# Layers 0 and 1 of a four-layer graph network: the second half's weight products as seven half products per pair of tiles, statistics on ScalarE, a bias added by transfers

## The chip, the cores and the metric

The kernel runs on one core of a Trainium2 chip, in float32. The metric is the device time of one execution, in microseconds (us); less is better. One launch computes everything, and nothing is computed on the host but the reordering of inputs.

## The reference

Four layers run one after the other on `x` (2708 x 512) with one adjacency matrix `adj` (2708 x 2708, positive weights with the diagonal set). Each layer normalizes, mixes the rows by the matrix, multiplies by a 512 x 512 weight and adds the result to `x`:

```
h = relu(layernorm(x));  x = x + relu(norm(adj + I) @ h @ W0)            # layer 0
h = relu(layernorm(x));  x = x + (norm(adj) @ h @ W1.T + b1)             # layer 1
h = relu(layernorm(x));  x = x + relu(norm(adj + I) @ h @ W2)            # layer 2
h = relu(layernorm(x));  x = x + sigmoid(ga * (attn @ h @ Wsa)           # layer 3
                                       + gb * (adj @ h @ Wg + bg))
```

`norm` scales rows and columns by the inverse roots of the row sums; `attn` is a masked softmax over scores of pairs of nodes; `ga`, `gb` are sigmoid gates.

## The kernel before

**Tiles.** The 2708 rows are 20 full tiles of 128 rows (five for each quarter of the rows, `KT = 5`) and two tail tiles with what is left, 22 in all (`NT`). The first half `H1` is tiles 0 to 9; the second half `H2` is tiles 10 to 19 and the two tails. `h` holds the normalized rows of all tiles in SBUF. `agg` holds the aggregated rows (matrix times `h`), transposed, for one layer.

**A layer.** `aggregate` runs `outer_product(p)` for p = 1, 7, 2, 4, 6, 5, 3 (a product of quarter blocks with seven products in the place of eight, done twice, once in each other). For each p and each half `u` of the columns it loads four blocks of the matrix (`load_o`, on SP's queue, 847.5 KB each) into places taken from the list `free`, makes sums of them on VectorE (`inner_y`: t1, t2, t4 into three buffers and t3 in place) and of parts of `h` (`inner_x`), and runs seven products of ten matmul instructions on TensorE (`multiply`, lines 541 and 547). `free` is a queue of seven places in `obuf`: each use takes four from its front and puts them back at its end, so the next use begins with those that have been free for longest. `aggregate` calls `epilogue(H1)` ahead of the last outer product and `epilogue(H2)` after it; then the next layer's first outer product follows. That one needs `h` of the tiles in `H1` only.

**The epilogue.** `next_x` goes through the tiles in groups of three. For a tile it loads the kept `x` (`load_x`, line 916, on POOL's queue), multiplies the aggregated tile by the weight (`project`, then `tile_product`: four products of 128x128 by 128x512, line 203, each shown as two instructions), applies scale and ReLU on ScalarE (line 929) or scale and `b1` on VectorE (line 931), adds `x` on VectorE (line 934), writes the new `x` to DRAM (line 935, POOL) and takes mean and variance on VectorE (`stats`, lines 234 and 235). For each group it works out the inverse root (`rstd_of`, lines 239 to 230, with one square root on ScalarE, line 224) and normalizes on ScalarE (line 255). A tail's operand is first gathered by copies on VectorE (line 181) into one of two scratch places `y_places`, which are handed out in turn by `new_y`; the ReLU's output takes one of them too.

**Order.** The framework puts each engine's instructions in an order ahead of time: for each engine the earliest in the program that is ready by its reckoning goes next, so program order is the priority, and work of a later stage fills what it holds to be gaps. On the chip every engine then takes its queue in that order.

**Products by pairs.** Layer 3 has the other form of weight product in `gated`, for both halves. `weights_of_pairs` makes four sums of quarter weights (VectorE, once). For a pair of tiles `sums_of_pair` makes four sums of 128x256 on VectorE (lines 1065 to 1068), and `pair_product` runs seven products of two 128x128 by 128x257 products (line 1077) with one copy on ScalarE (line 1088) and five additions on VectorE (lines 1092, 1098, 1103, 1107, 1110):

```
part(pa, 1); v = copy(pa);  part(pb, 6); u2 = v + pb
part(pa, 2, added);         part(pc, 7); u3 = u2 + pc
part(pd, 5); c22 = u3 + pd
part(pc, 4, added); c21 = u2 + pc
part(pd, 3, added); c12 = u2 + pd
results: first tile [pa, c12], second tile [c21, c22]
```

`v`, `u2`, `u3`/`c21` and `c22` live in `upool` (two buffers for `u2`, one for the others); `pa`, `pc`, `pd` share five PSUM banks (`gates_bank`), `pb` has two of its own.

## Time and profile before

| What | Value |
|---|---|
| Time, median of three runs | 2078.27 us (2078.13 to 2078.53) |
| The profiled execution's own time | 2074.84 us |
| Its span (first to last instruction) | 2073.0 us |
| TensorE busy | 2027.9 us, 98% of the span |
| VectorE busy | 1495.6 us, 72% |
| ScalarE busy | 406.1 us, 20% |
| POOL busy | 202.2 us, 10% |
| Granted TensorE clock | 0.997 |

Engines are PE (TensorE), PEld (its weight load), DVE (VectorE), ACT (ScalarE), POOL and SP; an engine with a q behind it is its queue of transfers. A row of the groups view reads: line, engine, operation, output<-input, shapes, count | busy us in all, mean ns of one | idle time ahead of it and what ended it. Matmul instructions overlap, so that their mean is more than the time from one start to the next. In the windows view each line is a stretch of time in us from the span's start, its length, and the busy time and number of instructions of each engine, then the granted clock and what the transfers did. In the timeline a line is start, duration, engine, line, operation and, in brackets, the idle time ahead and its releaser. Layer 0's epilogue of `H2` begins at 413.16 us, layer 1's at 793.71 us; layer 3's products by pairs of the first half lie from 1489.72 to 1520.67 us.

### The profile page before, as it was taken

How to read it: one execution, taken by the hardware profiler on the slowest of the kernel's cores; microseconds unless marked ns; L12 is line 12 of the kernel's file. 1: busy time of each engine (PE TensorE's matmuls, PEld its weight loads, DVE VectorE, ACT ScalarE, POOL GpSimd, SP SyncE). 2: the span in 40 equal slices, each digit the busy share in tenths (PEclk: the TensorE clock that was granted, in tenths of full speed). 3: DMA queues.
4: the chain of work that ended last, by engine and by line, in shares of the span. 5: the costliest groups of instructions: out<-in, count | busy, mean ns of one | idle time of the engine just before them, and what ended most of it. 6: DMA issues, size and time to landing. Idle time of an engine off the chain costs nothing.

```text
span 2073.0 us, 20307 instructions
## 1 busy us (share of the span) xinstructions
PE 2027.9 (98%) x7338; PEld 1285.3 (62%) x7338; DVE 1495.6 (72%) x2593; ACT 406.1 (20%) x822; POOL 202.2 (10%) x367
## 2 busy tenths in 40 slices
PE   5999999999999999999999999999999999999998
PEld 2566655646666655666664556666677666676665
DVE  4678877756776777766587889967758876677634
ACT  1340001130000010100002130000026434444411
POOL 0111111120000011100002130001011000001012
PEclk9999999999999999999999999999999999999999
DMA  9998595555545444754454565545543333233221
GB/s 368 306 376 256 179 338 188 192 184 178 181 148 182 145 167 145 237 179 160 162 169 145 202 210 201 170 157 178 179 149 116 118 105 104 95 105 118 93 82 52
DMA packets 81332, 363.69 MB, mean 175 GB/s; under 512 B 11616, under 2 KB 16668, under 8 KB 81104
## 3 DMA queue, kind: packets, MB, share of 16 engines
q1 hardware_dynamic: 50672, 245.43, 34.5%
q0 software_dynamic: 30560, 116.97, 17.5%
q8 instruction: 58, 0.95, 0.2%
q14 instruction: 42, 0.34, 0.0%
HBM read 297.39 MB, written 62.19 MB: 173 GB/s over the span
## 4 chain that ended last, share of the span: by engine, by line
PE 88%; DVE 5%; DMA 4%; issue 1%; ACT 0%; POOL 0%; SPq 0%; POOLq 0%; DVEq 0%; ACTq 0%
PE pe L1359 17%; PE pa L541 14%; PE pc L541 14%; PE pd L541 14%; PE po L203 9%; PE pb L541 7%; PE pt L603 3%; DMA obuf<-in_yb_dram 2%; PE pd L1077 2%; PE pa L1077 2%; PE pc L1077 1%; DMA ends<-in_yt_dram 1%; PE pt L608 1%; PE pe L603 1%; PE pb L1077 1%
## 5 line engine op out<-in xcount | busy, mean ns | idle before, releaser
L1359 PE MATMUL pe<-obuf,h 128*128 128x339 f32 x1280 | 373.2, 448 | 0.0
L541 PE MATMUL pa<-obuf,h 128*128 128x339 f32 x1040 | 318.7, 451 | 2.5 <-ACT h L255 1.4
L1359 PEld LDWEIGHTS pe<-obuf,h 128*128 128x128 f32 x1280 | 241.4, 189 | 121.8 <-issue 4.1
L541 PEld LDWEIGHTS pa<-obuf,h 128*128 128x128 f32 x1040 | 196.2, 190 | 110.2 <-issue 10.3
L203 PE MATMUL po<-ends,agg 128*128 128x512 f32 x480 | 207.5, 593 | 0.0
L1225 ACT ACTIVATE e<-r,nsr 128x339 f32<-128x339 f32 x352 | 172.4, 566 | 178.2 <-DVE obuf L1229 87.1
L541 PE MATMUL pb<-t,s 128*128 128x339 f32 x560 | 171.0, 452 | 0.8 <-DVE t L513 0.8
L541 PE MATMUL pc<-t,h 128*128 128x339 f32 x560 | 169.4, 448 | 1.3 <-DVE u L588 1.3
L541 PE MATMUL pd<-t,s 128*128 128x339 f32 x560 | 169.0, 447 | 0.0
L541 PE MATMUL pd<-obuf,s 128*128 128x339 f32 x550 | 166.3, 448 | 1.1 <-DVE s L557 0.8
L575 ACT COPY v<-pa 128x339 f32<-128x339 f32 x56 | 24.7, 441 | 719.0 <-PE pa L541 693.0
L203 PEld LDWEIGHTS po<-ends,agg 128*128 128x128 f32 x480 | 90.9, 190 | 114.3 <-issue 109.5
L541 PEld LDWEIGHTS pb<-t,s 128*128 128x128 f32 x560 | 106.3, 191 | 56.1 <-DVE t L513 2.1
L541 PEld LDWEIGHTS pc<-t,h 128*128 128x128 f32 x560 | 105.8, 189 | 56.3 <-DVE u L588 2.4
L541 PEld LDWEIGHTS pd<-t,s 128*128 128x128 f32 x560 | 105.8, 189 | 54.1
L541 PEld LDWEIGHTS pd<-obuf,s 128*128 128x128 f32 x550 | 104.0, 189 | 54.8 <-DVE s L557 1.3
L541 PE MATMUL pc<-obuf,s 128*128 128x339 f32 x450 | 135.9, 448 | 0.0
L541 PEld LDWEIGHTS pc<-obuf,s 128*128 128x128 f32 x450 | 85.1, 189 | 43.8 <-issue 0.5
L935 POOL DMA_DIRECT2D xs<-ends x66 | 36.0, 545 | 780.9 <-DVE ends L934 702.2
L513 DVE TENSOR_TENSOR t<-obuf,t 128x1695 f32<-128x1695 f32 x55 | 105.2, 1913 | 0.0
L1229 DVE SCALAR_TENSOR_TENSOR obuf<-obuf,e 128x1695 f32<-128x1695 f32 x32 | 61.5, 1923 | 58.8 <-DMA obuf<-in_yb_dram 39.8
L514 DVE TENSOR_TENSOR t<-obuf,t 128x1695 f32<-128x1695 f32 x52 | 99.4, 1912 | 0.5 <-PE pc L541 0.5
(321 smaller groups left out, 2417.4 us busy)
## 6 DMA issues: line engine op xcount, KB each, us to landing
obuf<-in_yb_dram SPq DMA_DIRECT2D x132, 847.5 KB, 4.6
obuf<-osumt SPq DMA_DIRECT2D x100, 847.5 KB, 4.5
osumt<-obuf POOLq DMA_DIRECT2D x22, 847.5 KB, 12.1
xs<-ends POOLq DMA_DIRECT2D x66, 256.0 KB, 2.3
ends<-xs POOLq DMA_DIRECT2D x60, 256.0 KB, 4.1
obuf<-in_yt_dram SPq DMA_DIRECT2D x28, 339.0 KB, 3.6
obuf<-in_yb_dram POOLq DMA_DIRECT2D x11, 847.5 KB, 10.8
ends<-in_yb_dram SPq DMA_DIRECT2D x9, 847.5 KB, 9.4
```

Source lines behind the costliest of these rows:

```text
L203: nc.tensor.matmul(po, cs[c], ws[c], start=(c == 0), stop=(c == NC - 1))
L513: nc.vector.tensor_add(t2, o22, t1)
L514: at_y.append(nc.vector.tensor_add(t4, o21, t2).ins)
L541: last = nc.tensor.matmul(ps, x[:, k, :], y[:, k, :], start=start and k == 0, stop=k == KT - 1, skip_group_check=not start,)
L575: at_v.append(nc.scalar.copy(v, pa).ins)
L603: nc.tensor.matmul(ps[c], h[:, NF, c * P : (c + 1) * P], tl[:, 0, :], start=start, stop=False)
L608: nc.tensor.matmul(ps[c], h[g, NF + 1, c * P : (c + 1) * P], tl[g, 1, :], start=False, stop=True)
L935: nc.gpsimd.dma_start(xs[t], xt)
L1077: nc.tensor.matmul(ps, xs_[k][:, c], ws[k][:, c], start=start and c == 0, stop=c == 1, skip_group_check=not start,)
L1225: nc.scalar.activation(e[:, k], row, AF.Exp, bias=nsr[:, t, s : s + 1], scale=1.0)
L1229: nc.vector.scalar_tensor_tensor(b, b, 0.0, e1[:, :n], ALU.not_equal, ALU.min)
L1359: nc.tensor.matmul(pe[c], h[:, t, c * P : (c + 1) * P], a, start=(t == 0), stop=False)
```

## The change

For layers 0 and 1, and for the second half only, the ten full tiles are projected as five pairs by `next_x_by_pairs`; the two tails go through `next_x` after them, as a group of two. The sums of the weights, the sums of the pairs and one more place for a kept `x` lie in three blocks taken from the front of `free`, which are put back at its end when the epilogue is done. ScalarE takes sum and sum of squares (`stats_by_act`) for all of these tiles in layer 1, and in layer 0 for all but the second tile of every second pair. `b1` is no longer loaded to SBUF and added on VectorE: in layer 1's aggregation 22 transfers on POOL's queue add `b1` to the kept `x` in DRAM (after outer product 1 for `H1`, after 7 for six tiles of `H2`, after 2 for the other six), and in both epilogues of layer 1 the scaled product is added to `x` in one instruction. `weights_of_pairs`, `sums_of_pair` and `pair_product` are unchanged; the function definitions only move in the file.

```diff
+    def places_of_pairs():
+        blks = [free.pop(0) for _ in range(3)]
+        flat = [blk.rearrange("p k w -> p (k w)") for blk in blks]
+        n = 2 * D
+        return (
+            blks,
+            [flat[0][:, k * D : (k + 1) * D] for k in range(3)] + [flat[1][:, 0:D]],
+            [in_four(flat[1][:, D : D + n]), in_four(flat[2][:, 0:n])],
+            flat[2][:, n : n + D],
+        )
+
+    def stats_by_act(xt, mv):
+        y = new_y()
+        nc.scalar.activation(y, xt, AF.Identity, accum_out=mv[:, 0:1])
+        nc.scalar.activation(mv[:, 0:1], mv[:, 0:1], AF.Copy, scale=1.0 / D)
+        nc.scalar.activation(y, xt, AF.Square, bias=mv[:, 0:1], scale=-1.0, accum_out=mv[:, 1:2])
+        nc.scalar.activation(mv[:, 1:2], mv[:, 1:2], AF.Copy, scale=1.0 / D)
+
+    def next_x_by_pairs(ts, w_sb, scale, relu, src, colscale, after=None):
+        nonlocal xt_places
+        blks, w_places, s_places, x_place = places_of_pairs()
+        xt_places = xt_places + [x_place]
+        ws = weights_of_pairs(
+            w_sb.rearrange("p c (k o) -> p c k o", k=2),
+            [a.rearrange("p (c o) -> p c o", c=NC // 2) for a in w_places],
+        )
+        halves = [slice(k * (D // 2), (k + 1) * (D // 2)) for k in range(2)]
+        pairs = [(t, t + 1) for t in ts if t < NF][::2]
+        xs_ = sums_of_pair(pairs[0], s_places)
+        for n, pair in enumerate(pairs):
+            xts = [load_x(t, src) for t in pair]
+            mv = small.tile([P, KT, 2], FP, tag="mv", name="mv")
+            *_, po = pair_product(xs_, ws, gates_bank)
+            if n + 1 < len(pairs):
+                xs_ = sums_of_pair(pairs[n + 1], s_places)
+            for s, (t, xt) in enumerate(zip(pair, xts)):
+                y = new_y()
+                for f, c in zip(halves, po[s]):
+                    if relu:
+                        nc.scalar.activation(y[:, f], c, AF.Relu, scale=scale[:, t : t + 1])
+                    else:
+                        nc.vector.scalar_tensor_tensor(
+                            xt[:, f], c, scale[:, t : t + 1], xt[:, f], ALU.mult, ALU.add
+                        )
+                if relu:
+                    nc.vector.tensor_add(xt, xt, y)
+                nc.gpsimd.dma_start(xs[t], xt)
+                if s == 0 or n % 2 == 0 or not relu:
+                    stats_by_act(xt, mv[:, s, :])
+                else:
+                    stats(xt, mv[:, s, :])
+            rstd = rstd_of(mv, 2)
...
+        xt_places = [p for p in xt_places if p is not x_place]
+        next_x([t for t in ts if t >= NF], w_sb, scale, relu, src, colscale, after)
+        free.extend(blks)
...
     def next_x(ts, w_sb, scale, relu, src, colscale, after=None):
...
-                if bias is None:
-                    nc.scalar.activation(y, po, AF.Relu, scale=scale[:, t : t + 1])
-                else:
-                    nc.vector.scalar_tensor_tensor(
-                        y, po, scale[:, t : t + 1], bias, ALU.mult, ALU.add
-                    )
-                nc.vector.tensor_add(xt, xt, y)
+                if relu:
+                    y = new_y()
+                    nc.scalar.activation(y, po, AF.Relu, scale=scale[:, t : t + 1])
+                    nc.vector.tensor_add(xt, xt, y)
+                else:
+                    nc.vector.scalar_tensor_tensor(
+                        xt, po, scale[:, t : t + 1], xt, ALU.mult, ALU.add
+                    )
...
-    b1_bc = misc[:, 0:D]
-    nc.gpsimd.dma_start(b1_bc, b1.partition_broadcast(P))
-    aggregate(False, lambda ts: next_x(ts, w1_sb, dis, b1_bc, xs, dinv))
+    def add_b1(ts):
+        for t in ts:
+            nc.gpsimd.dma_start(xs[t], b1.partition_broadcast(P), accum_op=ALU.add)
+    aggregate(
+        False,
+        lambda ts: (next_x if ts[0] < half else next_x_by_pairs)(
+            ts, w1_sb, dis, False, xs, dinv
+        ),
+        {p: lambda ts=ts: add_b1(ts) for p, ts in zip((1, 7, 2), (H1, H2[:6], H2[6:]))},
+    )
```

## The prediction

> **What bounds the kernel now.** I read the page first (engines, the 40 slices), then the windows view of the stretches that the change touches, then the timeline around them, and last the groups view, for durations.
>
> ```profile
> PE 2027.9 (98%) x7338; PEld 1285.3 (62%) x7338; DVE 1495.6 (72%) x2593; ACT 406.1 (20%) x822; POOL 202.2 (10%) x367
> ...
> core 0: us, PE busy (x) PEld busy (x) DVE busy (x) ACT busy (x) POOL busy (x), PEclk, DMA share, GB/s
> 413.16:447.50 34.34, 34.34 (x82) 15.20 (x81) 19.92 (x56) 11.24 (x18) 8.01 (x15) 1.00 0.38 132
> 793.71:828.10 34.39, 34.39 (x82) 15.25 (x81) 26.37 (x67) 5.06 (x9) 8.15 (x15) 1.00 0.40 137
> 1489.72:1520.67 30.95, 30.95 (x144) 26.35 (x141) 21.39 (x64) 11.79 (x31) 4.37 (x8) 1.00 0.27 96
> ```
>
> The first two windows are the ten full tiles of `H2` in layers 0 and 1, the third is the ten tiles of layer 3's `gated`, which already go by pairs. TensorE has no gap in either stretch to be changed, at full clock, so only less TensorE work can shorten them. VectorE has 14.4 us free in layer 0 and 8.0 in layer 1, ScalarE 23 and 29. A product stage of 140 short instructions has run once, in 30.95 us, with VectorE at 69%.
>
> ```profile
> 399.57 1.92 DVE L512 TENSOR_TENSOR t<-obuf 128x1695 f32<-128x1695 f32 x1
> 401.53 1.93 DVE L516 TENSOR_TENSOR obuf<-obuf 128x1695 f32<-128x1695 f32 x1
> ...
> 409.24 1.92 DVE L513 TENSOR_TENSOR t<-obuf,t 128x1695 f32<-128x1695 f32 x1
> ...
> 411.49 1.91 DVE L514 TENSOR_TENSOR t<-obuf,t 128x1695 f32<-128x1695 f32 x1
> ...
> 413.36 43.32 SPq L445 DMA_DIRECT2D obuf<-in_yb_dram  x2
> ...
> 1501.62 0.42 DVE L1107 TENSOR_TENSOR u<-u,pc 128x257 f32<-128x257 f32 x1
> 1501.95 0.42 DVE L1138 TENSOR_TENSOR ends<-pa,ends 128x256 f32<-128x256 f32 x1
> ...
> L255 ACT ACTIVATE h<-ends,sh,rstd 128x512 f32<-128x512 f32 x66 | 49.1, 804 | 35.4 <-DVE sh L247 35.1
> L929 ACT ACTIVATE ends<-po,dd 128x512 f32<-128x512 f32 x44 | 30.2, 685 | 169.0 <-PE po L203 167.1 <-PE po L210 1.8
> L286 ACT ACTIVATE y<-h,mv 128x512 f32<-128x512 f32 x12 | 8.7, 723 | 0.3
> L291 ACT ACTIVATE y<-h 128x512 f32<-128x512 f32 x12 | 7.6, 630 | 13.9 <-DMA h<-in_x_dram 13.6
> L224 ACT ACT_TABLE_LOAD x1 | 1.3, 1283 | 0.0
> ```
>
> The first four rows are the sums of the next layer's first outer product, made before this epilogue starts. The SPq row is two of the four loads for its second half. The two rows at 1501 us show that VectorE's 0.42 us operations follow each other every 0.33 us.
>
> **TensorE.** Removed: 80 instructions of 512 columns, 34.34 us, 0.43 each. Added: 140 of 256 columns. Layer 3's took 30.95 us for 257 columns, its own short stalls included; times 256/257 that is 30.8. Gain 3.5 us for a layer, 7.0 for both. With no stall at all (0.2169 from start to start in the timeline, as 0.8675 for four) it would be 30.3, and 8.1 for both: more than that the change can't bring.
>
> **VectorE, layer 0.** For the five pairs: 45 operations of 256 columns (nine a pair) by 0.335 = 15.1; ten additions of `x` (L934, 0.69, next one after 0.61) 6.1; statistics of two tiles left 1.6; five root chains of eight small operations, 0.2 each where each waits for the last and 0.09 where others lie between, 3.6 to 8.0; what is left over from outer product 3 at 413.3 to 415.5, 2.3. Sum 28.7 to 33.1, against 19.9 now and 30.8 of TensorE. Layer 1: 15.1, twenty half tiles by 0.40 (nearest row L1250, 0.48) 8.0, roots 3.6 to 8.0, left over 2.8: 29.5 to 33.9, against 26.4. The four sums of the weights (0.69 each by L934, 2.8) are needed by the second product, but their places have been free since outer product 3's first half, and VectorE is busy only 13.4 of 20 us ahead of 413; I cost them at nothing, and at 2.8 if that cover is gone.
>
> **ScalarE, layer 0.** A pair: the copy `v` 0.3; four half ReLUs, between the copy of 256 columns (0.36) and L255's 256 columns with two operands (0.59), I take 0.37 apart, 1.5; statistics of a tile 0.75 and 0.84 (L291 and L286 with their reads of the sum) and two scalings of 0.2, 2.0; two normalizations at 0.74, 1.5; a root 0.2. That is 7.5 with two statistics and 5.5 with one, 33.5 for five pairs. Some 6 of it fall behind the last product, which leaves 27.5 of 30.8. Layer 1 has no ReLU: 30, of which 24.5 fall inside. So all three engines are nearly full.
>
> **A rule against it.** The chip loaded a table three times in the whole profile; L224's load came with the first square root at 30.6 us, and the sums and squares of 80 to 110 us and every later root, ReLU and copy went on without one. The Trainium skill (ScalarE: Activation LUTs, What ACT_TABLE_LOAD costs) says that every switch to another table set costs some 2.66 us. If Square and Identity were not in the square root's set, each pair would pay two switches, 5.3 us, and ScalarE would pace layer 0 at about 12 us a pair, some 25 us a layer lost. The trace decides: square, then root, without a load, so nothing.
>
> **What moves.** Three blocks leave `free`. The next layer's first half then no longer gets the three that had long been free, but those that outer product 3's second half releases last, the fourth only at 413.2. So t2, t3 and t4 (three of the four rows above, 1.92 each, 5.8 us) move behind 413 into the full VectorE. They are first needed by product `pb` of the next layer, which starts at 456.16 now. The transfers themselves (4.6 us to landing) have 35 us to arrive. The second half's blocks (three behind the last pair, at about 444, on SP in order) are needed by its sums near 462; now too one of them, the second transfer of the SPq row above, is sent only at 456.35; t3 began with it at 464.18 and TensorE never waited. So nothing.
>
> **The tails** now wait: a tail's gather takes a `y` place that the last pair still uses. Behind the last product come c12 0.5, ReLU 0.55, addition 0.8, the second tile's ReLUs 0.9 and addition 0.8, copies 0.9, about 4.5 us, in layer 1 as much through the statistics. TensorE has the next layer's `pa` in hand meanwhile, 2.86 us, and `pb` if t2 is ready. Between 0 and 1.6 us a layer; I take 0.5.
>
> **POOL and transfers.** 22 accumulating transfers of 256 KB. Nearest rows: accumulations of 847.5 KB cost POOL 0.86 us and land in 10.8; plain ones of 256 KB cost 0.54 and land in 2.3 to 4.8. POOL pays 12 to 19 us of its 1870 idle us. Queued behind one that waits are POOL's `x` loads, which have several free places ahead of their use, and the writes of `x`: nothing. Between gain and loss nothing is excluded (the load of `b1` goes away, 5.6 MB of writes come); I take nothing, up to 4 us if they delay matrix blocks.
>
> **H1 of layer 1** saves ten additions, 6.1 us of VectorE, where TensorE is busy 35.00 of 35.00: nothing.
>
> **Sum.** -7.0, plus stalls inside the pairs beyond layer 3's, because VectorE and ScalarE have about 95% to carry: 0 to 2.5 a layer, 0.7 taken, 1.4; plus 1.0 for the tails. -4.6 us. Against the profiled execution, 2074.84 (span 2073.0), that is 2070.2; the median shown, 2078.27, lies 3.4 above that execution, and I carry the difference over: 2073.7. About 0.2%, 4.2 us, is what a measurement can tell from no change.
>
> **The rivals.**
> B: ScalarE paces layer 0. The second tile's ReLU shares a `y` place with the first one's addition, normalizations are older in program order, and `u3` (one buffer) waits until that ReLU has read it; then product 4 waits about 1 us a pair. Layer 0 gives 0, layer 1 2: about 2076.5. For: 33.5 against 30.8. Against: layer 3's trace shows TensorE running 6, 7 and 5 ahead of a late 2.
> C, slower: VectorE becomes the bound. From 413.16 to `pb` it must do 33.1 + 5.8 + 6.3 for the tails (copies, additions, statistics, root), 45.2, and 48 with the weight sums. It decides when this exceeds the 43.0 us that TensorE takes there now. A t of 1.92 us put into a gap of 0.3 holds up the whole queue behind it. Price 2 to 5 us a layer: 2082 to 2088, likeliest 2083. Against: the t's are later in program order, and behind the pairs VectorE was busy only 11.3 of 20 us, so it can catch up.
> D: `b1`'s ten first transfers fall on 452 to 472, where transfers take 0.80 of their engines, and matrix blocks come late: 4 us on top, 2078.
> E: the order does not interleave pairs, and each pair begins with sums after the last addition, 1 us a pair: gain 0 in both layers, 2078. Against: in layer 3 the sums of the next pair stand between the additions of this one.
>
> **How the numbers follow.** The likeliest case 0.54 (its own range 2071 to 2076; 0.46 of it faster, 0.08 within); B 0.16 (0.01 faster, 0.13 within, 0.02 slower); C 0.20, slower; D and E 0.10 (0.07 within, 0.03 slower). Faster 0.47, within 0.28, slower 0.25. The range goes from the stall-free 2070.2 to C's likely value, 2083, and leaves out the worse half of C.
>
> **What would show it.** Right: 140 instructions of 256 columns in 31 to 32.5 us in each layer, TensorE busy throughout, VectorE 29 to 33 us in it, no new table load, `pb` of the next layer 3 us earlier. Wrong: over 34 us with PE waiting for `u` or `s` (VectorE) or `v` (ScalarE); rows L513, L514 or L516 between the pairs' additions; PE waiting for `t` at the next layer's `pb`; blocks from DRAM landing late beside the `b1` transfers.

## The result, and the profile after

The changed kernel takes 2103.97 us (median of four runs, 2101.79 to 2106.65), the kernel before 2078.2, measured beside it: ratio 1.0128, 95% interval 1.0115 to 1.0142. That is 26 us slower where 4.6 us less were forecast, and outside the range. The profiled execution took 2106.65 us, its span is 2104.9 us. The engines on its page:

```profile
PE 2034.0 (97%) x7458; PEld 1311.9 (62%) x7458; DVE 1503.8 (71%) x2675; ACT 442.0 (21%) x954; POOL 221.2 (11%) x388
```

The two profiled executions differ by more than the medians: their spans are 31.9 us apart (2104.9 - 2073.0). TensorE is busy for 6 us more although its matmuls have less to do, and idle for 26 us more (2104.9 - 2034.0 against 2073.0 - 2027.9). The windows view of the two stretches of pairs, from their first product to the one behind their last, layer 0 and layer 1 (start:end, length, then busy time of each engine, granted clock, DMA share, GB/s):

```profile
416.75:454.83 38.08, 35.34 (x153) 28.21 (x152) 31.19 (x85) 23.16 (x67) 10.00 (x15) 1.00 0.55 137
819.18:852.00 32.82, 32.72 (x146) 26.93 (x144) 30.41 (x92) 19.31 (x57) 7.55 (x14) 1.00 0.39 128
```

Each window also holds a few instructions of other products: by the timeline they take 1.7 us of the second (a tail's product) and 3.6 us of the first (the next layer's first products). So layer 1's pairs take 31.1 us, as forecast, and TensorE is idle for 0.1 us there. Layer 0's take 34.5 us, no less than the 34.34 they replace. Neither explains the loss. It is found by cutting the time at the first products of the epilogues: from layer 0's second-half epilogue to layer 1's first-half one, on to its second-half one, and on to layer 2. First three lines of before, then three of after:

```profile
413.16:719.28 306.12, 306.12 (x1068) 190.02 (x1066) 214.14 (x328) 28.85 (x48) 13.72 (x25) 1.00 0.51 170
719.28:793.71 74.43, 74.43 (x224) 41.81 (x221) 53.95 (x108) 8.96 (x16) 10.86 (x20) 1.00 0.48 164
793.71:1104.34 310.63, 309.41 (x1083) 191.62 (x1082) 223.82 (x339) 21.78 (x38) 17.00 (x31) 1.00 0.52 172
```

```profile
416.75:743.53 326.78, 310.49 (x1127) 203.01 (x1126) 226.67 (x372) 45.38 (x113) 24.03 (x36) 0.98 0.56 176
743.53:819.18 75.65, 74.69 (x224) 41.71 (x221) 47.89 (x106) 9.07 (x16) 11.30 (x21) 1.00 0.39 130
819.18:1130.84 311.66, 307.01 (x1144) 203.46 (x1142) 226.88 (x374) 41.17 (x105) 16.35 (x30) 0.99 0.53 179
```

20.7 of the 31.9 us are lost in the first of these, almost all of it behind the pairs, in the tails and layer 1's outer products: TensorE is idle for 16.3 us of the stretch, and the clock falls to 0.98. The other two lose 1.2 and 1.0 us, what follows them 5.4, and what lies ahead of them 3.6. 2.1 of these 3.6 us are one gap that ends at 382.36 us, while the first `b1` transfers run; e2_b1_only (below) has such a gap too, and the kernel before, e1_no_b1 and e5_few_rows have none there. The timeline of TensorE after shows two of the holes (start, duration, engine, line, and in brackets the idle time ahead and who ended it):

```profile
468.65 5.37 PE L203 MATMUL po<-ends 128*128 128x512 f32 x8 [4.51 <-DVE ends L181]
...
485.56 0.94 PE L541 MATMUL pd<-obuf,s 128*128 128x339 f32 x1 [4.60 <-DVE agg L562]
```

Both name VectorE, and VectorE's own timeline passes the blame on to blocks of the matrix that have not landed:

```profile
464.01 1.93 DVE L512 TENSOR_TENSOR t<-obuf 128x1695 f32<-128x1695 f32 x1 [6.00 <-DMA obuf<-in_yb_dram]
...
468.28 0.36 DVE L181 COPY ends<-agg 128x128 f32<-128x128 f32 x2
...
484.37 0.30 DVE L463 SCALAR_TENSOR_TENSOR obuf<-ident,obuf 128x128 f32<-128x128 f32 x1 [8.17 <-DMA obuf<-osumt]
```

And POOL, in the same stretch, stands at the transfers of `b1` (L1105), with the writes of `x` (L1041) and the loads of `x` (L989) behind them:

```profile
445.90 0.84 POOL L1105 DMA_DIRECT2D xs<-in_b_dram  x1 [5.08 <-DMA xs<-ends]
...
462.50 0.85 POOL L1105 DMA_DIRECT2D xs<-in_b_dram  x1 [9.32 <-DMA xs<-ends]
463.06 0.86 POOL L1041 DMA_DIRECT2D xs<-ends  x1
463.61 0.85 POOL L1041 DMA_DIRECT2D xs<-obuf  x1
```

The transfers of `b1`, meant for layer 1's products, were put as early as their data allow: behind each write of `x` in layer 0's epilogue. The last row writes the `x` that lies in a block of `obuf`; that block can be loaded anew only when the write has landed. SP's queue sends the last block of layer 1's first product then:

```profile
469.36 0.33 SPq L445 DMA_DIRECT2D obuf<-in_yb_dram  x1
```

Three more of them go at 449.6, 452.5 and 455.0 us. Before, one block of that product was sent after 414 us:

```profile
456.35 0.33 SPq L445 DMA_DIRECT2D obuf<-in_yb_dram  x1
```

So the first theory was: what costs is the place of these transfers at the head of POOL's queue. Its rivals were the blocks that change hands, the bytes of the transfers, and full engines in the pairs.

### The profile page after: what moved, and what is told of

The parts are those of the page before. It is cut to its first block, busy times and chain, and to the rows that moved or that the text cites. A ratio compares the mean times of both kernels' runs of the same rounds, so it can differ in the third digit from the quotient of the medians.

```text
span 2104.9 us, 20810 instructions
## 1 busy us (share of the span) xinstructions
PE 2034.0 (97%) x7458; PEld 1311.9 (62%) x7458; DVE 1503.8 (71%) x2675; ACT 442.0 (21%) x954; POOL 221.2 (11%) x388
## 3 DMA queue, kind: packets, MB, share of 16 engines
q0 software_dynamic: 33648, 122.48, 19.2%
## 4 chain that ended last, share of the span: by engine, by line
PE 74%; issue 11%; DMA 6%; DVE 5%; POOL 2%; ACT 1%; POOLq 0%; SPq 0%; DVEq 0%; ACTq 0%
PE pe L1435 17%; PE pc L541 12%; PE pa L541 12%; PE pd L541 12%; PE pb L541 6%; PE po L203 4%; PE pt L603 3%; DMA obuf<-in_yb_dram 2%; DMA obuf<-osumt 1%; PE pd L943 1%; PE pa L943 1%; PE pc L943 1%; PE pe L603 1%; PE pt L608 1%; DMA xs<-ends 1%
## 5 line engine op out<-in xcount | busy, mean ns | idle before, releaser
L541 PE MATMUL pa<-obuf,h 128*128 128x339 f32 x1040 | 316.5, 449 | 4.6 <-ACT v L575 3.2
L541 PEld LDWEIGHTS pa<-obuf,h 128*128 128x128 f32 x1040 | 195.8, 190 | 110.3 <-issue 6.9
L541 PE MATMUL pc<-t,h 128*128 128x339 f32 x560 | 171.4, 452 | 6.3 <-DVE u L588 6.2
L541 PE MATMUL pb<-t,s 128*128 128x339 f32 x560 | 172.7, 454 | 2.1 <-DVE s L473 1.3
L541 PE MATMUL pd<-obuf,s 128*128 128x339 f32 x550 | 168.6, 453 | 4.9 <-DVE agg L562 4.9
L575 ACT COPY v<-pa 128x339 f32<-128x339 f32 x56 | 24.5, 438 | 699.8 <-PE pa L541 696.8
L541 PE MATMUL pd<-t,s 128*128 128x339 f32 x560 | 169.4, 448 | 0.0
L541 PEld LDWEIGHTS pc<-t,h 128*128 128x128 f32 x560 | 106.4, 191 | 63.2 <-DVE u L588 9.2
L541 PEld LDWEIGHTS pb<-t,s 128*128 128x128 f32 x560 | 106.4, 191 | 59.1 <-issue 3.1
L541 PEld LDWEIGHTS pd<-obuf,s 128*128 128x128 f32 x550 | 105.0, 192 | 59.9 <-DVE agg L562 6.8
L541 PEld LDWEIGHTS pd<-t,s 128*128 128x128 f32 x560 | 105.8, 189 | 55.0 <-issue 1.3
L203 PE MATMUL po<-ends,agg 128*128 128x512 f32 x320 | 138.6, 593 | 0.0
L541 PE MATMUL pc<-obuf,s 128*128 128x339 f32 x450 | 135.9, 448 | 0.0
L541 PEld LDWEIGHTS pc<-obuf,s 128*128 128x128 f32 x450 | 85.1, 189 | 43.8 <-issue 0.5
L203 PEld LDWEIGHTS po<-ends,agg 128*128 128x128 f32 x320 | 60.5, 190 | 76.6 <-issue 73.9
L513 DVE TENSOR_TENSOR t<-obuf,t 128x1695 f32<-128x1695 f32 x55 | 105.4, 1916 | 0.1
L512 DVE TENSOR_TENSOR t<-obuf 128x1695 f32<-128x1695 f32 x48 | 92.1, 1919 | 14.6 <-DMA obuf<-in_yb_dram 11.6
## 6 DMA issues: line engine op xcount, KB each, us to landing
obuf<-in_yb_dram SPq DMA_DIRECT2D x132, 847.5 KB, 4.5
obuf<-osumt SPq DMA_DIRECT2D x100, 847.5 KB, 4.5
osumt<-obuf POOLq DMA_DIRECT2D x22, 847.5 KB, 11.0
obuf<-in_yb_dram POOLq DMA_DIRECT2D x11, 847.5 KB, 11.1
ends<-in_yb_dram SPq DMA_DIRECT2D x9, 847.5 KB, 9.8
```

Source lines behind the costliest of these rows:

```text
L203: nc.tensor.matmul(po, cs[c], ws[c], start=(c == 0), stop=(c == NC - 1))
L512: nc.vector.tensor_add(t1, o12, o11)
L513: nc.vector.tensor_add(t2, o22, t1)
L541: last = nc.tensor.matmul(ps, x[:, k, :], y[:, k, :], start=start and k == 0, stop=k == KT - 1, skip_group_check=not start,)
L575: at_v.append(nc.scalar.copy(v, pa).ins)
```

## The experiments

The table gives ratios to the kernel before, run beside each. One thousandth is 2.1 us. The ratios, not the medians, are compared between runs. e1, e7, e8, e9 and e12 leave `b1` out and e5 most of it; they are there to part causes.

| Run | What differs | Ratio, 95% interval |
|---|---|---|
| changed | | 1.0128, 1.0115 to 1.0142 |
| e1_no_b1 | changed, no `b1` transfers | 1.0022, 1.0013 to 1.0032 |
| e2_b1_only | before, with the `b1` transfers | 1.0091, 1.0065 to 1.0118 |
| e3_b1_late | changed, transfers behind the last write of `x` | 1.0168, 1.0138 to 1.0198 |
| e4_turned | before, `free` turned by three | 0.9996, 0.9987 to 1.0005 |
| e5_few_rows | changed, transfers cut to 8 rows | 1.0019, 1.0010 to 1.0029 |
| e6_b1_spread | changed, transfers spread over layer 1 | 1.0059, 1.0042 to 1.0077 |
| e7_layer1_only | no `b1`, pairs in layer 1 alone | 1.0008, 0.9999 to 1.0017 |
| e8_no_x_place | no `b1`, no place of `x` in a block | 1.0009, 1.0000 to 1.0019 |
| e9_tails_early | e8, tails behind the first pair | 1.0031, 1.0017 to 1.0045 |
| e10_b1_pool | e9, `b1` added by POOL and VectorE | 1.0048, 1.0035 to 1.0061 |
| e11_layer0_early | e9's pairs in layer 0 alone, layer 1 as before | 1.0034, 1.0021 to 1.0048 |
| e12_one_block | e8, pairs hold one block instead of three | 0.9980, 0.9971 to 0.9990 |
| e13_layer0_one_block | e12's pairs in layer 0 alone, layer 1 as before | 1.0001, 0.9991 to 1.0010 |
| e14_ten_by_transfer | e12, `b1` by ten spread transfers and VectorE | 0.9993, 0.9986 to 1.0000 |

### The transfers of b1: there or not, alone, later

e1_no_b1 takes the hooks out of the changed kernel:

```diff
-        {p: lambda ts=ts: add_b1(ts) for p, ts in zip((1, 7, 2), (H1, H2[:6], H2[6:]))},
```

> The changed kernel without its 22 transfers of b1 (b1 is left out of the computation; everything else stays). My theory: these transfers stand at the head of POOL's in-order queue, each waiting for the write of the x that it adds to, and so hold up the later writes and loads of x, the place of x that lies in a block of obuf, and with it the next layer's blocks. Then about 25 of the 26 us that the change lost come back and the time is 2072 to 2080 us; the start of the first-half epilogue of layer 1, 743.60 us in the changed kernel, goes back to 716 to 722, and TensorE has no gap over 2 us between 414 and 600 us. Rival 1, the blocks: free hands over its places in another order and one place of x lies in a block of obuf, which alone makes the next layer's blocks late; then the gaps at 464, 481 and 505 us stay and the time is 2095 to 2104. Rival 2, bandwidth: only the bytes of b1's transfers count; then 6 to 10 us come back (2094 to 2098), since 11 MB in all are a small share of what is moved. Rival 3, full VectorE and ScalarE in the pairs: less than 5 us come back.

Measured: 2082.3 us, 1.0022. Of 1.0128, 1.06%, or 22 us, are the transfers' doing. The remaining 0.22% (4.6 us) is not: the time lies 2 us above what my theory gave. One gap over 2 us stays between 414 and 600 us, 3.3 us at the tails. The two rivals that leave `b1` out of the cause fall.

e2_b1_only puts the same transfers into the kernel before, without pairs:

```diff
-            y, po, scale[:, t : t + 1], bias, ALU.mult, ALU.add
+            xt, po, scale[:, t : t + 1], xt, ALU.mult, ALU.add
...
+        for t in ts:
+            nc.gpsimd.dma_start(xs[t], b1.partition_broadcast(P), accum_op=ALU.add)
```

> The kernel before with only the b1 part of the change: 22 accumulating transfers on POOL's queue and, in layer 1's epilogues, the scaled product added to x in one instruction; no pairs, no blocks taken from free. My theory: POOL's queue is held up in the second-half epilogue of layer 0 here too, but with the two old places of x outside obuf the blocks do not hang on it, so that part of the loss shows: 5 to 20 us slower than before, 2083 to 2098, with waits of POOL at the transfers of b1 for the writes of x of several us each and x loads late at L916. Rival 1, the blocks alone: within 3 us of before. Rival 2, bandwidth: 6 to 10 us slower.

Measured: 2095.98 us, 1.0091, 19 us. Most of the loss comes without pairs and without a place of `x` in a block, so the chain through that block, which my theory had for a good part of it, isn't needed.

e3_b1_late holds all 22 back behind the last write of `x`:

```diff
+        with tc.issue_after(last_x):
             for t in ts:
                 nc.gpsimd.dma_start(xs[t], b1.partition_broadcast(P), accum_op=ALU.add)
```

> The changed kernel with all its transfers of b1, which are now put behind the last write of x of the layer before in POOL's order; nothing else is changed. My theory: what costs is their place in POOL's queue, not their bytes or their number; then the time is that of the kernel without b1 plus at most 3 us, 2072 to 2082 us, and the start of layer 1's first-half epilogue lies at 716 to 724 us. Rival 1, the blocks: 2095 to 2104, unchanged. Rival 2, bandwidth: the same bytes fall on the same layer, so at least 6 of the 10 us remain: 2082 to 2100.

Measured: 2110.78 us, 1.0168, slower still, and outside all three expectations. My theory falls. POOL's writes and loads of layer 0 were no longer held up (no gap over 1.4 us before 488), but the transfers then ran one behind the other from 470 to 525 us, beside the matrix blocks. The windows view of that time:

```profile
480.00:500.00 20.00, 10.37 (x33) 6.49 (x33) 7.19 (x10) 0.44 (x1) 4.05 (x6) 0.81 1.03 240
500.00:520.00 20.00, 20.00 (x66) 12.91 (x65) 13.00 (x14) 3.24 (x3) 6.40 (x8) 0.94 1.05 162
520.00:540.00 20.00, 11.29 (x34) 7.01 (x32) 8.15 (x10) 0.00 (x0) 4.12 (x7) 0.74 1.06 227
```

The DMA engines are full (share 1.03 to 1.06; before, 0.52 in each of these stretches), and they move no more than 162 to 240 GB/s, where the load of the kernel's first blocks reaches 370 (the rows of the 40 slices). TensorE waited 9.6 and 8.7 us for VectorE's L588, which stood behind late blocks. So the accumulating transfers are dear. The two DMA tables, POOL's queue of the changed kernel and of e1_no_b1 (packets, MB, share of 16 engines):

```profile
q0 software_dynamic: 33648, 122.48, 19.2%
```

```profile
q0 software_dynamic: 30480, 116.71, 17.1%
```

19.2% of 2104.9 us less 17.1% of 2081.1 us is 48 us of all 16 engines for 22 transfers, 2.2 us each (e2_b1_only against before gives 1.8, e6_b1_spread against e1_no_b1 2.3). The rest of this queue moves 116.7 MB in 356 us, 0.8 us for 256 KB. A `b1` transfer takes the engines two to three times as long as this queue's average for the same bytes. No run tells which property makes it so: that it adds, that it goes from DRAM to DRAM, or that its source is one row read 128 times. How much of a packet's time is waiting beside other transfers the traces do not tell either.

### Bytes or queue

e5_few_rows leaves the 22 transfers where they are in POOL's queue, with their waits, and cuts what they carry:

```diff
-            nc.gpsimd.dma_start(xs[t], b1.partition_broadcast(P), accum_op=ALU.add)
+            nc.gpsimd.dma_start(xs[t][0:8], b1.partition_broadcast(8), accum_op=ALU.add)
```

> The changed kernel with each of its 22 transfers of b1 cut to the first 8 of a tile's 128 rows (b1 is left out of the other rows). They stand at the same places of POOL's queue and wait for the same writes of x, but carry 16 KB for 256 KB. Theory Q, POOL's queue: the waits at its head are what costs, so nearly all of the loss stays, 2096 to 2104 us. Theory D, the DMA engines: 256 KB that are accumulated in DRAM take them twice as long as 256 KB that are plainly written (from the queues' shares of before and after, 1.7 us of all 16 engines against 0.8), 37 us in all, in a stretch that has room for half of that; then nearly all of it goes and the time is 2082 to 2088, near that of the kernel without b1 (2082.3).

Measured: 2080.22 us, 1.0019, the same as with no transfers at all, and 2 us below theory D's range; theory Q falls. POOL still stands at them, first the changed kernel's waits, then this one's (us in total, times, longest):

```profile
POOL xs L1105 <- DMA xs<-ends: 91.1, 15, 15.7
```

```profile
POOL xs L1105 <- DMA xs<-ends: 43.5, 14, 8.6
```

43.5 us of waiting at the head of POOL's queue cost nothing that the times show. What the changed kernel pays for is the bytes, that is the time that 256 KB take in the DMA engines. That POOL's longer waits are a consequence of it, since the writes that it waits for land late, fits these rows but was not tested by itself.

e6_b1_spread carries all bytes but one transfer at a time, behind every second matrix block:

```diff
+        t = b1_due.pop(0) if b1_due else None
+        if t is not None:
+            with tc.issue_after(at_sp.ins):
+                nc.sync.dma_start(bs[t][0], b1)
+            with tc.issue_after(at_x[-1]):
+                nc.gpsimd.dma_start(xs[t], bs[t][0].partition_broadcast(P), accum_op=ALU.add)
```

> The changed kernel with its 22 full transfers of b1 spread out over layer 1: the transfer of one tile follows every second matrix block from the first product's second half to the fifth product (each waits for a 2 KB copy of b1 that stands on SP's queue behind that block's load). Theory D: the same 37 us of DMA time then meet 230 us in which the engines are half idle (share 0.52), so the loss goes: 2080 to 2087, as without b1, and the granted clock stays at 1.00 from 490 us on. Theory Q: POOL's queue is held for longer still, the loads of x of layer 1 come late, and the time is 2095 or more.

Measured: 2089.4 us, 1.0059, between the expectations and nearer to theory D's: 14 of the 22 us come back although POOL waits 153.8 us for the copies, and 7.7 stay. The share is 0.74 to 0.80 from 480 to 540 us:

```profile
480.00:500.00 20.00, 17.07 (x54) 10.84 (x53) 12.59 (x18) 1.64 (x2) 3.98 (x6) 0.91 0.74 229
500.00:520.00 20.00, 20.00 (x71) 13.24 (x70) 14.11 (x15) 2.04 (x3) 2.29 (x3) 1.00 0.80 217
```

A block beside such a transfer still comes late now and then (gaps of 2.9 us up to 489.7 and 1.9 up to 616.4, and slower instructions after each). Even spread, the transfers are not free; what the 22 small copies on SP's queue cost, which this run adds, was not measured. Some 2.7 us of the rest lie at the very end of the program (last section).

### What the pairs lose without b1

e4_turned turns the order of places in the kernel before:

```diff
+        if turned:
+            free.extend([free.pop(0) for _ in range(3)])
```

> The kernel before with free turned by three places behind the second-half epilogues of layers 0 and 1, as if three blocks had been taken from its front and put back at its end; nothing else. It shows what the handing on of other places costs by itself. My theory and the prediction: within 2 us of before, 2076 to 2080, with the three sums of 1.92 us of the next layer's first product moved behind the epilogue's start. Rival 1, the blocks: TensorE waits 2 to 5 us a layer for the sums or the second half's blocks, 2082 to 2090.

Measured: 2075.73 us, 0.9996: nothing. The sums moved behind 413 us (L513 now at 418.25) and TensorE did not notice.

e7_layer1_only (without the hooks, and `next_x` for all of layer 0):

```diff
-        (next_x if ts[0] < half else next_x_by_pairs)(ts, w_sb[0], dinv, True, x, dis)
+        next_x(ts, w_sb[0], dinv, True, x, dis)
```

> The kernel without b1, with pairs in layer 1 alone; layer 0's second half goes tile by tile as before (b1 is left out). It parts the 6 us that the kernel without b1 still lies over the kernel before. My theory: in layer 0 the place of x that lies in a block of obuf comes free only when the x is written, the block's load is late by 3 to 5 us, VectorE stands at the sum of that block with the last tile's addition behind it, and the idle TensorE then runs its next 3 us at a lower clock; layer 1 gains 0.4 as it is. So 2074 to 2077 us, 6 to 8 less than the kernel without b1. Rival, VectorE and ScalarE too full in both layers alike: 2078 to 2080. Rival, the pairs gain nothing and the tails cost the same in both: 2079.

Measured: 2079.18 us, 1.0008. Both rivals' figures fit, my theory's do not, and the interval touches both no difference from before and that of e1_no_b1, so the times alone do not part the layers. The profile does: layer 1 to 2 took 312.5 us (310.6 before), with gaps of 2.5 us at the tails and 2.6 behind them. So the fault is not layer 0's alone, as I had it.

e8_no_x_place:

```diff
-        xt_places = xt_places + [x_place]
```

> The kernel without b1 and without the additional place of x in a block of obuf; pairs in both layers (b1 is left out). My theory, the block of the next layer waits for the write of that x: the block's load starts 3 us earlier, at about 453.5 instead of 456.8, the gap of 3.3 us ahead of layer 0's tails goes down to less than 1.5 and the slow clock behind it goes too: 2075 to 2079 us. Rival, the other two blocks are as late (they are held by the last pair's products) or the pairs now wait for places of x: 2081 to 2085.

Measured: 2079.81 us, 1.0009 (the intervals of this and of e1_no_b1 overlap). In the profile the last block of layer 1's first product is sent at 450.2 instead of 456.4 us, and layer 0's gap at the tails is 0.9 for 3.3 us; but layer 1 has one of 3.3 us there, where VectorE stood at a late block before it came to the tail's copies:

```profile
833.37 0.61 DVE L463 SCALAR_TENSOR_TENSOR obuf<-ident,obuf 128x45 f32<-128x45 f32 x3 [2.53 <-DMA obuf<-in_yb_dram]
...
837.20 0.44 DVE L181 COPY ends<-agg 128x32 f32<-128x32 f32 x4 [0.49 <-ACT ends L1009]
```

In the windows view, from each second-half epilogue to the next first-half one, TensorE is idle for 3.6 and 3.8 us:

```profile
412.71:720.76 308.05, 304.50 (x1127) 200.92 (x1126) 224.28 (x368) 45.06 (x113) 13.78 (x25) 1.00 0.52 177
796.03:1106.35 310.32, 306.54 (x1143) 203.20 (x1141) 226.90 (x374) 41.41 (x105) 16.97 (x31) 0.99 0.53 181
```

e9_tails_early asks whether it is the tails:

```diff
+            if n == 0:
+                next_x([t for t in ts if t >= NF], w_sb, scale, relu, src, colscale, after)
...
-        next_x([t for t in ts if t >= NF], w_sb, scale, relu, src, colscale, after)
```

> The kernel without b1 and without the place of x in obuf (b1 is left out), in which the two tails are projected behind the first pair instead of behind the last. It tests what still eats the pairs' gain: there TensorE stood 0.9 us in layer 0 and 3.3 us in layer 1 ahead of the tails (L181), because the copies that gather a tail stood on VectorE behind the sums and loop additions of a block of the next layer that came late, and behind statistics on ScalarE. My theory: both gaps go, and layer 0 from its second-half epilogue to layer 1's first-half one takes 305 to 307 us (306.1 before, 308.05 with the tails last), layer 1 to 2 306 to 308 us (310.6 before, 310.3 with the tails last): 2071 to 2075 us, 0.1 to 0.3% below before. Rival: the late block stops another user of VectorE just as long (the next layer's u2 and u3), and TensorE waits there: 2077 to 2081, no gain.

Measured: 2083.89 us, 1.0031: the rival, and worse than that. The gaps at the tails moved to the next layer's third sum (`u3`, L588), 2.4 us in layer 0 and 4.9 in layer 1. VectorE ahead of it, in layer 1:

```profile
846.81 1.93 DVE L512 TENSOR_TENSOR t<-obuf 128x1695 f32<-128x1695 f32 x1 [1.49 <-DMA obuf<-in_yb_dram]
...
850.60 0.41 DVE L463 SCALAR_TENSOR_TENSOR obuf<-ident,obuf 128x45 f32<-128x45 f32 x2 [1.78 <-DMA obuf<-in_yb_dram]
...
855.85 0.69 DVE L1137 CUSTOM_DVE_ANT_0 ends<-ends 128x512 f32<-128x512 f32 x1 [1.91 <-DMA ends<-in_wsa_dram]
856.54 0.50 DVE L588 TENSOR_TENSOR u<-u,pc 128x339 f32<-128x339 f32 x1
```

VectorE waits for one late block after the other, and whatever is queued behind their sums is late, a tail or a `u3`. The tails were only the first in line. The last wait of the four rows is for no block: it is for a part of layer 3's weight, whose use the order had put ahead of this `u3`. e7_layer1_only has such a wait too, 4.72 us (`in_asa_dram`), ahead of its gap of 2.6 us.

e12_one_block takes the blocks' holder away. The pairs hold one block; the rest of their sums lies in rows of `h` that nobody reads any more:

```diff
-        blks = [free.pop(0) for _ in range(3)]
+        blks = [free.pop(0)]
...
+            [flat[:, n : n + D], h[:, NF], h[:, NF + 1], h[:, NF - 2]],
+            [in_four(flat[:, 0:n]), in_four(hf[:, (NF - 4) * D : (NF - 2) * D])],
```

> The kernel without b1 and without the place of x in obuf (b1 is left out), tails last as in the change, in which the pairs take one block of free instead of three: two sums of weights lie in h of the tails, one in h of tile 18, and the second places of the pairs' sums in h of tiles 16 and 17, all of which are dead until these tiles are normalized. My theory, late blocks: with three blocks the next layer's second half could load its blocks only from the last pair's products on, and TensorE waited behind VectorE for them (3.6 us idle in layer 0 and 3.8 in layer 1 from the second-half epilogue to the next first-half one); with one it loads three of four as early as before, as the kernel before does, so the idle time falls to 1.5 to 2.5 in layer 0 (the 1.4 us stall inside the pairs stays) and under 1 in layer 1: 2070 to 2075 us, 2 to 6 below the one with three blocks. Rival, the tails: the late statistics on ScalarE and the shared places y hold up the gather whatever the blocks do, 3 us in layer 1 stay: 2077 to 2080.

Measured: 2072.82 us, 0.9980 (0.9971 to 0.9990), as expected: by the ratios 6 us less than with three blocks and 4 us less than the kernel before. Two blocks of the next layer's first product are sent only near the end of the pairs or behind them (446.5 and 450.7 us in layer 0, 825.2 and 831.5 in layer 1) where e8_no_x_place sends four (443.9 to 450.2 and 822.1 to 833.6); I had expected one. The windows of the same stretches:

```profile
413.92:719.55 305.63, 303.15 (x1128) 200.82 (x1126) 223.83 (x369) 44.61 (x113) 13.77 (x25) 1.00 0.51 173
793.99:1101.34 307.35, 305.42 (x1144) 202.81 (x1142) 225.18 (x370) 40.90 (x105) 16.92 (x31) 1.00 0.52 177
```

Layer 1 takes 307.35 us for 310.63, a gain of 3.3 for one layer where the prediction had 3.5 for TensorE's work alone. Layer 0 gains 0.5. TensorE's idle time is 2.5 us in layer 0, as forecast, and 1.9 in layer 1, more than the 1 us forecast. In layer 0 it is made up differently: the wait of 1.4 us inside the pairs, which I thought would stay, is gone, and a gap of 2.1 us is there at the second tail. Its operand waits for a copy on ScalarE (L208), and that one for VectorE, which had stood 3.1 us for another block:

```profile
464.36 0.65 DVE L463 SCALAR_TENSOR_TENSOR obuf<-ident,obuf 128x128 f32<-128x128 f32 x3 [3.12 <-DMA obuf<-osumt]
...
465.69 0.59 ACT L208 COPY ends<-po 128x512 f32<-128x512 f32 x1 [3.46 <-DVE ends L1068]
...
466.33 1.12 PE L210 MATMUL po<-ends,all_again 128*128 128x512 f32 x2 [2.08 <-ACT ends L208]
```

So of the 6 us between three blocks and one, some 2 go with the waits inside layer 0's pairs (2.3 us of idle TensorE with three blocks, 0.4 with one), which no late block makes (the first point of the next section); the rest lies outside them.

### Whole versions

These four compute `b1`. e10_b1_pool adds `b1` to the loaded `x` by POOL:

```diff
+            if not relu:
+                for xt in xts:
+                    nc.gpsimd.tensor_add(xt, xt, b1_bc)
```

> The same with b1, but not by transfers: for the ten full tiles of layer 1's second half POOL adds b1 to the loaded x in SBUF, for the other tiles VectorE adds it as in the kernel before. If POOL's ten additions hide beside TensorE: within 2 us of the kernel with the tails behind the first pair, 2072 to 2077, a whole version that may beat the one before. If POOL's queue is too late with the x (each addition waits for a load and stands ahead of the next loads and writes), or takes VectorE's time: 2080 to 2090, with PE waiting for VectorE at L1035's rows.

Measured: 2086.71 us, 1.0048, the second expectation. The 3 us above e9_tails_early are within the two intervals, and VectorE also adds `b1` for twelve tiles here, so that what POOL's additions cost the whole is not shown; what they do to VectorE beside them is (last section).

e11_layer0_early (its `b1` as before, layer 1 by `next_x`):

```diff
-        lambda ts: (next_x if ts[0] < half else next_x_by_pairs)(
-            ts, w1_sb, dis, False, xs, dinv
-        ),
+        lambda ts: next_x(ts, w1_sb, dis, False, xs, dinv),
```

> Pairs in layer 0 alone with the tails behind the first pair and no place of x in obuf; layer 1 is that of the kernel before, b1 on VectorE included. If layer 0's pairs gain what the kernel with the tails behind the first pair gains there: 2075 to 2077 us, within 0.1% of before. If the 1.4 us stall inside the pairs and the next layer's blocks eat it: 2078 to 2080.

Measured: 2084.79 us, 1.0034: more than either expectation, though its profiled execution (2080.51) lies 4 us below the median. In that profile the gaps of e9's layer 0 return, 2.8 us at the next `u3` among them.

e13_layer0_one_block is the same with e12's single block and the tails last again.

> Pairs in layer 0 alone with one block, tails last; layer 1 is that of the kernel before, b1 on VectorE included. A whole version. Late blocks: layer 0 from its second-half epilogue to layer 1's first-half one takes 303.5 to 305 us (306.1 before), 2075 to 2077. If the stall inside the pairs and the tails eat it: 2077 to 2080, no difference from before.

Measured: 2075.89 us, 1.0001: no difference from before, though time and layer 0 (304.75 us for 306.12 in its profile) lie in the ranges of the first expectation.

e14_ten_by_transfer has pairs in both layers with one block, and `b1` by transfers for ten tiles only:

```diff
+    b1_due += [None] * 8
+    for t in range(half, NF):
+        b1_due += [None, None, None, t]
```

> Pairs in both layers with one block; b1 by transfers for the ten full tiles of the second half alone, one behind every fourth matrix block of layer 1, and on VectorE for the other tiles as in the kernel before. A whole version. Ten accumulating transfers take 10 x 1.7 = 17 us of the DMA engines over some 160 us with a share of 0.52: hidden, so within 2 us of the kernel with one block and no b1, 2071 to 2077. Rival: each of them still delays the block beside it by 1 to 2 us, and layer 1's slack is too small for that: 2078 to 2083.

Measured: 2075.71 us, 0.9993 (0.9986 to 1.0000), within the expectation. By the ratios it is 28 us faster than the changed kernel, and its interval just touches that of no difference from the kernel before: a gain of 1.5 us at the likeliest, less than the 0.2% that the prediction called measurable. Against e12_one_block the ten transfers and the `b1` of the other tiles cost 2.7 us at the likeliest (the intervals touch), where 2 us were given.

## Why the prediction was wrong

Cutting the 26.6 us (1.28%) by the runs: the `b1` transfers 22.0 (changed to e1_no_b1; by e5_few_rows it is their bytes), the place of `x` in a block 2.7 (to e8_no_x_place; intervals that overlap), the other two blocks 6.0 (to e12_one_block; it takes the waits inside layer 0's pairs with it), and what is left is a gain of 4.2, with an interval from 2.1 to 6.0. The sum of the prediction was a gain of 4.6.

- **TensorE, VectorE, ScalarE, the rule.** Right in layer 1: 31.1 us for the pairs against 30.8 plus 0.7, VectorE 30.4 within 29.5 to 33.9, ScalarE 19.3 where 24.5 had been reckoned. Layer 0's pairs took 34.5 us, 3 more than reckoned, so that TensorE's term of 3.5 gave nothing there. 2.7 us of it is idle TensorE, in four waits, the longest of 1.37 us; that one is in every version that has layer 0's pairs with three blocks and in none with one. The changed kernel's timeline shows whom it waits for:

```profile
444.47 1.50 ACT L255 ACTIVATE h<-ends,sh,rstd 128x512 f32<-128x512 f32 x2
...
445.97 0.49 ACT L1034 ACTIVATE ends<-s,dd 128x256 f32<-128x256 f32 x1
...
446.49 0.69 DVE L1040 TENSOR_TENSOR ends<-ends 128x512 f32<-128x512 f32 x1 [1.48 <-ACT ends L1034]
447.10 0.41 DVE L969 TENSOR_TENSOR s<-u,pd 128x256 f32<-128x256 f32 x1
...
447.57 1.13 PE L943 MATMUL pd<-ends,obuf 128*128 128x256 f32 x4 [1.37 <-DVE s L969]
```

  Two normalizations of an earlier pair (L255) stand ahead of a ReLU on ScalarE, VectorE's addition of `x` waits for the ReLU, the next pair's `c22` (L969) stands behind the addition, and TensorE waits for `c22`. VectorE stands 1.48 us for such a ReLU at 439.02 us too, and TensorE 0.50 behind it. That is rival B's mechanism in the main, and its forecast for layer 0, no gain, came true for the pairs. With one block the instructions stand in another order, 0.4 us of idle time is left, and layer 0's pairs take 31.4 us (e12, 413.92 to 450.52 us less 5.2 us of other products). No pair switched ScalarE's tables: three loads in the whole profile, as before.
- **POOL and transfers, "I take nothing, up to 4 us".** This is the step that failed: it measures 22 us, of which some 2.7 lie at the program's end (last section). Its nearest row was there (accumulations of 847.5 KB landed in 10.8 us, plain blocks of the same size in 4.6), but I took POOL's 0.86 us of issuing for the cost and asked whether POOL had time, not whether the DMA engines had. 22 transfers at 2.2 us are 48 us of full engines; layer 1's products use 0.52 of them, so that they need at least 100 us of those, and even 230 us (e6_b1_spread) were not free of loss. Rival D had the right mechanism (transfers beside matrix blocks) with a price of 4 us and the wrong stretch: it counted ten transfers and the 20 us from 452 on.
- **"Queued behind one that waits ... nothing".** The transfers were put just behind the writes that they depend on, so they did stand ahead of later writes and loads. By e5_few_rows that order alone, with little to carry, costs nothing measurable.
- **What moves, "So nothing".** Wrong by some 7 us, in the second half of its paragraph: 8.7 from e1_no_b1 to e12_one_block, less the 2 us of waits inside layer 0's pairs. The first half (t2, t3, t4 behind 413) was right: e4_turned shows nothing. But "now too one of them is sent only at 456" set one late block against what became four, and VectorE waits for them one after the other with the last pair's and the tails' work queued behind. The profiles of e8 and e9 show these waits; e12 shows that the loss goes with the blocks. That t3's block was late already before (VectorE waited 2.62 us for it at 464.18, in the stretch that the prediction quotes) said that there was little room.
- **The tails, 0.5.** With one block TensorE is idle for 2.1 us ahead of the second tail in layer 0, and not at all at layer 1's tails. With three blocks (e8) the loss there, 1.3 us in two gaps and 3.3 us, came mainly from the late blocks (2.53 us of VectorE's wait in layer 1) and less from the shared `y` (0.49 us for ScalarE's statistics): with the tails early it only changed place.
- **H1 of layer 1, nothing.** A loss of 1.2 us in the changed kernel and in e1_no_b1 alike (75.7 for 74.4), of which 1.0 is a gap at L588 that goes away with one block.
- **Rival C** (VectorE the bound) ended on the right side but not for its reason: VectorE was not short of time, it stood waiting, for blocks and for ScalarE.

## What to carry to other kernels

A transfer that adds in DRAM is to be priced in time of the DMA engines, read from a row of the same kind, and laid against the share that the stretch has left; that its queue is idle says nothing. Scratch room borrowed from a rotating set of buffers is paid by whoever loads into it next: ask which blocks come late and what stands in the queue behind their first reader, and look for dead rows elsewhere. When a wait moves as the order is changed, as from the tails to `u3` here, look for its cause upstream of both.

## What was unexpected

- A short idle time of TensorE can cost more than itself. In the changed kernel ten instructions of L541 take 3.02 us as a rule. After gaps of 2.05 and 4.60 us they took 4.81 and 5.21, and after another gap of 2.06 us 3.12:

```profile
507.12 3.12 PE L541 MATMUL pc<-t,h 128*128 128x339 f32 x10 [2.06 <-DVE u L588]
...
530.03 4.81 PE L541 MATMUL pc<-t,h 128*128 128x339 f32 x10 [2.05 <-DVE u L588]
```

  The granted clock is 0.65 in the window of the second row (530.03 to 534.84 us), 0.58 in that of the 5.21 us (485.5 to 490.7), and 1.00 in that of the first (507 to 510). In e6_b1_spread a gap of 1.89 us was enough; in e11_layer0_early one of 2.77 us was not (3.13 us behind it). What decides between the two the traces do not show. The Trainium skill (TensorE: Matmul & The Clock Gate, the table in Why this matters for your kernels) warns of gaps over some 3 us; here shorter ones were followed by slow instructions too, though not each time.
- POOL's additions in SBUF hold up VectorE. In e10_b1_pool an addition of 128x512 takes 1.43 us in the mean, and one of VectorE's smallest operations beside it takes 1.23 where its median before is 0.16:

```profile
821.61 1.36 POOL L1027 TENSOR_TENSOR ends<-ends 128x512 f32<-128x512 f32 x1 [1.25 <-DMA ends<-xs]
821.76 1.23 DVE L227 TENSOR_TENSOR rq<-rstd 128x2 f32<-128x2 f32 x1
```

  The Trainium skill (SBUF — State Buffer, Who interferes with whom) says that a VectorE instruction with two inputs in SBUF contends with a POOL instruction that reads SBUF. These rows agree.
- The program's end grows with POOL's transfers. From the start of POOL's last row of writes of the output to the end of the span it takes 8.6 us without `b1` transfers (before, e1, e10 and e12), 9.0 with the 22 small ones, 10.0 with ten full ones and 11.3 to 11.4 with 22 (the changed kernel, e2, e3 and e6). So about 2.7 us of the loss come long after the transfers. What happens there the traces do not show; it stays open. Open too is why the stage from 1256.5 to 1463.6 us takes 1.8 us longer in the changed kernel (207.2 us for 205.3, from 1229.9 to 1435.2 before), of which one gap of 1.0 us is seen.
